# Last layer's experts: three projection pieces of 112, 112 and 64 + 64 columns, rows turned one part ahead, result reads in one row

## The chip, the core and the metric

The kernel runs on one core of a Trainium2 chip. A core has TensorE (PE; its weight loads are listed apart as PEld), VectorE (DVE), ScalarE (ACT), GpSimd (POOL) and SyncE (SP, which here only asks for transfers). They run at the same time and wait for each other through semaphores. The metric is the device time in microseconds (us) of one execution; lower is better. Everything is in fp32.

## What is computed

The program is a network of four layers on 4096 rows (16 sequences of 256) of 128 numbers. Each layer computes `x = x + s * silu(ffn(xn))`, where `xn` is the normalised `x`, `s` the output of the layer's mixer and `ffn` the layer's feed-forward part. The change touches only the feed-forward part of the last layer, a mixture of 16 experts with 2 experts per row and 640 places per expert, and one shared expert that all rows pass:

```python
def _mlp(h, wg, wu, wd):
    return jax.nn.silu(h @ wg) * (h @ wu) @ wd        # wg, wu: 128 x 176, wd: 176 x 128
...
expert_inputs = jnp.zeros((E, C, d), x.dtype).at[idx_flat, pos_c].add(x_pair)      # E = 16, C = 640
expert_outputs = jax.vmap(_mlp)(expert_inputs, w_gate, w_up, w_down)
gathered = expert_outputs[idx_flat, pos_c] * (vals_flat * within)[:, None]
output_tokens = gathered.reshape(N, K, d).sum(axis=1)
return x + _mlp(x, sw_gate, sw_up, sw_down) + output_tokens.reshape(b, s, d)
```

The hidden width is 176. An array of 128 columns takes it in two pieces.

## The kernel before

The last layer's mixer (a state-space scan, lines 1550 to 1960) ends at 3881 us. During it the rows of `xn` were already scattered to their experts' places in DRAM (`xd`, with the place to write back to and the router's weight in `md`). Then `ffn3` (line 1364) runs, in four stages:

- **Loads.** SP asks for the weights in groups (`weights`, lines 1374 to 1381: gate, up and down apart), for `mt`, and for the rows of the first experts (`rows_of`, line 1417; three buffers of 640 rows).
- **Shared expert** (lines 1427 to 1430). Eight chunks of 512 rows pass `mlp`; VectorE adds the result to `xn`.
- **Routed experts** (lines 1431 to 1446). Each expert's 640 rows are two parts: four tiles of 128 rows, and one. A part is transposed by TensorE into the PSUM tile `f3_pt` (line 1439), copied to SBUF by ScalarE as `f3_xT` (line 1441), passed through `mlp`, and scaled per row by VectorE into `f3_y` (line 1444). Then GpSimd issues five indirect writes, one for each 128 rows, to the rows' places in `yd` (`put_rows`, line 1359).
- **Tail** (lines 1449 to 1457). When all 80 indirect writes have landed, SP reads the two results of each row back in eight reads of 512 KB into `f3_r` (three buffers). For each, GpSimd adds the two (line 1454), VectorE adds `xn` (line 1455), and `gate` (lines 112 to 114) does silu on ScalarE, a product and a sum on VectorE; SP writes 256 KB of output.

`mlp` (lines 1383 to 1401) cuts the hidden width into two halves of 88, `j = 0, 1`. For each half one matmul makes the gate `pg` (line 1391) and one the up projection `pu` (line 1392), both with the half's 88 weight columns standing in the array and up to 512 rows streaming; ScalarE writes silu of `pg` to `h` (line 1393), VectorE multiplies `pu` into it (line 1394). Then for every 128 rows two matmuls, `j = 0` and `j = 1`, add up the down projection in `po` (line 1398): 88 rows of the array are used, 128 columns stream. An fp32 matmul appears in the trace as two passes, two LDWEIGHTS and two MATMUL records.

PSUM has eight banks here: two each for `f3_pg`, `f3_pu`, `f3_pt` and `f3_po`.

Nothing in `ffn3` fixes the order of instructions on an engine: the framework's scheduler sets it when the program is built. It prefers what is written first, but fills a wait that it foresees with later work that is ready. [...]

Of the kernel before, what the change touches and what calls it, by code (L numbers as in the profile page):

```python
# [8 lines left out]
F32 = mybir.dt.float32  # L9
AF = mybir.ActivationFunctionType  # L10
ALU = mybir.AluOpType
# [4 lines left out]
P = 128  # L16
B, S, D = 16, 256, 128
NT = B * S // P
NCH = B * S // 512
# [14 lines left out]
class Net:  # L34
# [1329 lines left out]
    def ffn3(self, xd, md, yd, sent):  # L1364


        nc, tc = self.nc, self.tc
        NE, F = 16, 88
        with ExitStack() as ctx:
            c = ctx.enter_context(tc.tile_pool(name="l3w", bufs=1))  # L1370
            sb = ctx.enter_context(tc.tile_pool(name="l3m", bufs=3))
            ps = ctx.enter_context(tc.tile_pool(name="l3m_ps", bufs=2, space=PSUM))

            def weights(lo, hi):

                t = []
                for n in ("wgate", "wup3", "wdown"):
                    src = self.a[n][:, lo:hi]
                    t.append(c.tile(list(src.shape), F32, name=f"{n}_{lo}"))
                    nc.sync.dma_start(t[-1], src)  # L1380
                return t

            def mlp(w, e, xT, n):

                wg, wu, wd = w
                h = sb.tile([F, 2, 512], F32, name="f3_h")
                for j in range(2):
                    f = slice(j * F, (j + 1) * F)
                    pg = ps.tile([P, 512], F32, name="f3_pg")
                    pu = ps.tile([P, 512], F32, name="f3_pu")  # L1390
                    nc.tensor.matmul(pg[:F, : n * P], lhsT=wg[:, e, f], rhs=xT, start=True, stop=True)  # L1391
                    nc.tensor.matmul(pu[:F, : n * P], lhsT=wu[:, e, f], rhs=xT, start=True, stop=True)  # L1392
                    nc.scalar.activation(h[:, j, : n * P], pg[:F, : n * P], AF.Silu)
                    nc.vector.tensor_tensor(h[:, j, : n * P], h[:, j, : n * P], pu[:F, : n * P], ALU.mult)
                po = ps.tile([P, 4, D], F32, name="f3_po")
                for k in range(n):
                    for j in range(2):
                        nc.tensor.matmul(  # L1398
                            po[:, k, :], lhsT=h[:, j, k * P : (k + 1) * P], rhs=wd[:, e, j, :], start=j == 0, stop=j == 1
                        )  # L1400
                return po

            sync = mybir.DependencyInfo(mybir.DependencyClass.Sync, mybir.DependencyReason.DATA)

            def fetch(out, src, scattered):
                d = nc.sync.dma_start(out, src)
                for q in scattered:
                    tc.add_manual_dep(d.ins, q.ins.name, sync, reason="scattered rows")

            shared = weights(NE, NE + 1)  # L1410
            mt = c.tile([P, NE, 5, 2], F32, name="f3_mt")
            fetch(mt, md[0 : 640 * NE, :].rearrange("(e p k) t -> p e k t", p=P, k=5), sent[1])
            to = c.tile([P, NE, 5], mybir.dt.int32, name="f3_to")
            nc.vector.tensor_copy(to, mt[:, :, :, 0])
            xs, ws, done = {}, {}, []

            def rows_of(e):
                x = xs[e] = sb.tile([P, 5, D], F32, name="f3_x")
                fetch(x, xd[640 * e : 640 * e + 640, :].rearrange("(p k) d -> p k d", k=5), sent[0])

            for e in range(2):
                if e == 0:
                    ws[0] = weights(0, 4)
                rows_of(e)
            for g in range(1, 4):
                ws[g] = weights(4 * g, 4 * g + 4)
            for t in range(NCH):
                k4 = slice(4 * t, 4 * t + 4)
                po = mlp(shared, 0, self.xnT[:, t * 512 : (t + 1) * 512], 4)
                nc.vector.tensor_tensor(self.xn[:, k4, :], po, self.xn[:, k4, :], ALU.add)  # L1430
            for e in range(NE):
                if e + 2 < NE:
                    rows_of(e + 2)
                x = xs.pop(e)
                y = sb.tile([P, 5, D], F32, name="f3_y", bufs=4)
                for k0, n in ((0, 4), (4, 1)):
                    pt = ps.tile([P, 4, P], F32, name="f3_pt")
                    for k in range(n):
                        nc.tensor.transpose(pt[:, k, :], x[:, k0 + k, :], self.ident)
                    xT = sb.tile([P, 512], F32, name="f3_xT")  # L1440
                    nc.scalar.copy(xT[:, : n * P], pt[:, :n, :].rearrange("p k d -> p (k d)"))
                    po = mlp(ws[e // 4], e % 4, xT[:, : n * P], n)
                    for k in range(n):
                        nc.vector.tensor_scalar_mul(y[:, k0 + k, :], po[:, k, :], mt[:, e, k0 + k, 1:2])
                for k in range(5):
                    self.put_rows(yd, to[:, e, k : k + 1], y[:, k, :], done)
            xo = self.out.rearrange("(k p) d -> p k d", p=P)
            back = yd[0 : 2 * B * S, :].rearrange("(p n j) d -> p n j d", n=NT, j=2)
            for t in range(NCH):
                k4 = slice(4 * t, 4 * t + 4)  # L1450
                r = sb.tile([P, 4, 2, D], F32, name="f3_r")
                fetch(r, back[:, k4], done)
                acc = sb.tile([P, 4, D], F32, name="f3_acc")
                nc.gpsimd.tensor_tensor(acc, r[:, :, 0, :], r[:, :, 1, :], ALU.add)
                nc.vector.tensor_tensor(acc, acc, self.xn[:, k4, :], ALU.add)
                self.gate(sb, acc, 4 * t, 4)
                nc.sync.dma_start(xo[:, k4, :], self.x[:, k4, :])


class Route3:  # L1460
# [4 lines left out]
    NE, CAP = 16, 640.0  # L1465
# [506 lines left out]
def layout(i):  # L1972
# [5 lines left out]
    i = {k: np.asarray(v) for k, v in i.items()}  # L1978
    p0, f0 = (lambda n: i["L0_attn_" + n]), (lambda n: i["L0_ffn_" + n])
    a = {"x": p0("x").reshape(B * S, D)}  # L1980
# [34 lines left out]
    for h in range(16):  # L2015
        o, m = 8 * h, h % 4
# [7 lines left out]
    p3, f3 = (lambda n: i["L3_attn_" + n]), (lambda n: i["L3_ffn_" + n])  # L2024
# [6 lines left out]
        a[d + "cb"], a[d + "dtb"], a[d + "D"] = (two(q(n))[:, :, 0] for n in ("conv_b", "dt_b", "D"))  # L2031
        a[d + "A"] = two(q("Alog")).reshape(P, 32)
    a["rw"], a["rb"] = f3("router_w"), row(f3("router_b"))
    for n, o in (("gate", "wgate"), ("up", "wup3")):
        a[o] = np.concatenate([f3("w_" + n), f3("sw_" + n)[None]], 0).transpose(1, 0, 2)
    a["wdown"] = np.concatenate([f3("w_down"), f3("sw_down")[None]], 0).reshape(17, 2, 88, D).transpose(2, 0, 1, 3)
    return {k: np.ascontiguousarray(v) for k, v in a.items()}


# [15 lines left out]
```

## Time and profile before

Three runs: 4092.97 us median (4090.22 to 4107.63).

| | |
|---|---|
| profiled execution, own time | 4101.38 us |
| its span from first to last instruction | 4099.7 us |
| granted TensorE clock over the span | 0.956 |
| span before `ffn3` (mixer's last write) | 0 to 3881 us |
| shared expert | 3881 to 3926 us |
| routed experts | 3926 to 4060 us |
| tail | 4060 to 4099.7 us |

In the rows of the profile, `L1391` is a line of the kernel. `f_pg<-f_xT,wgate 128*88 128x512` reads: from `f_xT` and `wgate` into `f_pg`; 128 rows and 88 columns of the array, 512 elements streamed. Brackets give the time that the engine was idle just before, and what ended it. In the timeline, consecutive instructions of one kind on one engine are merged (`x4`). The end of a matmul is modelled (a pass of 512 columns is given 592 ns though the next one starts 429 ns later), so the starts are what can be read.

| in `ffn3` | count | mean of one |
|---|---|---|
| gate and up matmul passes, 512 columns, routed (L1391, L1392) | 128 | next start after 0.43 us |
| the same, 128 columns | 128 | next start after 0.11 us |
| down passes, 128 columns (L1398) | 448 | next start after 0.11 us |
| silu of 512 columns (L1393, ACT) | 48 | 592 ns |
| product of 512 columns (L1394, DVE) | 48 | 684 ns |
| copy of transposed rows, 512 columns (L1441, ACT) | 16 | 585 ns |
| scaling of 128 rows (L1444, DVE) | 80 | 345 ns |
| indirect write of 128 rows (L1359, POOL) | 80 | 957 ns, and 0.30 us to the next |
| addition of two results (L1454, POOL) | 8 | 1403 ns |

### The profile page before, as it was taken

The numbers are of one execution on the slowest core, as the hardware profiler recorded it, in microseconds if no ns is written. First come the engines' busy times: TensorE is split into PE (matmuls) and PEld (weight loads), VectorE is DVE, ScalarE is ACT, GpSimd is POOL, SyncE is SP. The second block draws the span as 40 slices with busy tenths as digits, with TensorE's granted clock in tenths as the row PEclk, the third lists the DMA queues.
The fourth block names the chain that finished last, engine by engine and source line by source line (L and its number), as shares of the span: only waits on it lengthen the run. The fifth ranks groups of instructions, "written<-read, shape, count | busy, mean of one in ns | idle before, by whom it ended". The sixth has DMA issues, their size and how long they took to land. (4 is left out here: it accounts for less than half of the span.)

```text
span 4099.7 us, 61363 instructions
## 1 busy us (share of the span) xinstructions
PE 3617.1 (88%) x21623; PEld 2311.1 (56%) x21623; DVE 2983.6 (73%) x6273; ACT 2125.9 (52%) x4623; POOL 1914.6 (47%) x1932
## 2 busy tenths in 40 slices
PE   5689999875999999899999899998888889889895
PEld 3467777553566666677777677665333333333363
DVE  5567677575788887666666666757899899999834
ACT  2356666642777776344545333343566566566322
POOL 5974444000444444333333200121888988877634
PEclk8899999986999999999999999998999999999898
DMA  8365555320000000100000300000111121121123
GB/s 304 127 210 188 199 181 193 42 79 6 1 1 1 1 1 1 42 1 1 1 1 1 115 2 1 3 25 23 66 66 66 67 87 67 67 83 62 58 77 102
DMA packets 87366, 268.90 MB, mean 66 GB/s; under 512 B 18176, under 2 KB 34088, under 8 KB 81555
## 3 DMA queue, kind: packets, MB, share of 16 engines
q1 hardware_dynamic: 80403, 255.46, 18.4%
q0 software_dynamic: 6656, 9.52, 0.7%
q8 instruction: 172, 2.82, 0.3%
q14 instruction: 135, 1.11, 0.1%
HBM read 192.96 MB, written 71.97 MB: 65 GB/s over the span
## 5 line engine op out<-in xcount | busy, mean ns | idle before, releaser
L1829 POOL TENSOR_TENSOR m_h<-m_B,m_dtu 128x1024 f32<-128x1024 f32 x256 | 597.6, 2358 | 111.2 <-PE m_y L1959 62.0
L1855 DVE TENSOR_TENSOR_SCAN m_h<-m_a,m_h 128x512 f32<-128x512 f32 x512 | 600.8, 1207 | 43.9 <-ACT m_a L1844 34.8
L1959 PE MATMUL m_y<-m_h,ident 128*128 128x512 f32 x1024 | 519.5, 637 | 20.8 <-DVE m_h L1955 20.7
L883 POOL TENSOR_TENSOR a_e<-a_e,a_sm 128x512 f32<-128x512 f32 x256 | 263.5, 1040 | 448.3 <-DVE a_sm L882 354.5
L1118 DVE SCALAR_TENSOR_TENSOR f_acc<-f_po,f_gate,f_acc 128x128 f32<-128x128 f32 x1024 | 287.4, 344 | 164.3 <-PE f_po L1113 154.3
L1959 PEld LDWEIGHTS m_y<-m_h,ident 128*128 128x128 f32 x1024 | 185.7, 196 | 340.4 <-issue 251.0
L1113 PEld LDWEIGHTS f_po<-values_sb,f_h 128*128 128x128 f32 x2048 | 273.0, 195 | 158.9 <-issue 133.0
L398 DVE TENSOR_TENSOR a_e<-a_s,a_c 128x384 f32<-128x384 f32 x256 | 216.4, 846 | 191.2 <-PE a_s L395 188.5
L1190 POOL TENSOR_TENSOR r_g<-r_t 128x256 f32<-128x256 f32 x256 | 183.5, 728 | 359.3 <-DVE r_t L1189 356.0
L1221 ACT ACTIVATE r_e<-r_s,r_mx 128x256 f32<-128x256 f32 x512 | 207.4, 473 | 259.7 <-DVE r_mx L1215 259.7
L1955 DVE TENSOR_TENSOR m_h<-m_h,m_C 128x1024 f32<-128x1024 f32 x256 | 306.6, 1198 | 28.4 <-PE m_C L1865 28.4
L1083 ACT ACTIVATE f_h<-f_ph 128x512 f32<-128x512 f32 x256 | 152.1, 596 | 328.9 <-PE f_ph L1081 314.3
L1189 DVE TENSOR_TENSOR r_t<-r_pp,trig_sb 128x512 f32<-128x512 f32 x256 | 169.1, 681 | 207.3 <-PE r_pp L1180 206.1
L1113 PE MATMUL f_po<-values_sb,f_h 128*128 128x128 f32 x2048 | 276.8, 279 | 26.3 <-ACT f_h L1083 13.4
L876 ACT ACTIVATE a_e<-a_e,a_mx 128x256 f32<-128x256 f32 x512 | 255.0, 500 | 54.6 <-DVE a_sm L882 48.2
L1081 PE MATMUL f_ph<-xnT_sb,keys_sb 128*128 128x512 f32 x512 | 269.8, 610 | 0.4 <-ACT f_gate L1048 0.4
L403 ACT ACTIVATE a_e<-a_e,a_mx 128x128 f32<-128x128 f32 (+1 forms) x512 | 218.9, 453 | 87.7 <-DVE a_mx L399 62.0
L1209 PE MATMUL r_s<-pe_sb,r_g 128*128 128x256 f32 x1024 | 259.0, 386 | 0.0
L373 POOL COPY a_st<-a_p 128x192 f32<-128x192 f32 x256 | 135.1, 530 | 244.5 <-PE a_s L394 161.6
L1844 ACT ACTIVATE m_a<-m_dt,bA_sb 128x510 f32<-128x510 f32 x256 | 170.9, 686 | 141.3 <-DVE m_h L1855 140.4
L1865 PE MATMUL m_C<-m_dbc,ident 32*128 32x512 f32 x512 | 152.7, 670 | 99.0 <-DVE m_h L1955 91.2
L1844 ACT ACTIVATE m_a<-m_dt,fA_sb 128x510 f32<-128x510 f32 x256 | 169.9, 685 | 110.2 <-DVE m_h L1855 109.3
(476 smaller groups left out, 8199.1 us busy)
## 6 DMA issues: line engine op xcount, KB each, us to landing
m_B<-m_rows SPq DMA_DIRECT2D x32, 2048.0 KB
a_p<-pc SPq DMA_DIRECT2D x32, 768.0 KB
a_c<-cs SPq DMA_DIRECT2D x32, 768.0 KB
cs<-a_es SPq DMA_DIRECT2D x64, 256.0 KB
pc<-a_es SPq DMA_DIRECT2D x64, 256.0 KB
a_p<-pc SPq DMA_DIRECT2D x32, 512.0 KB
a_c<-cs SPq DMA_DIRECT2D x32, 512.0 KB
cs<-bg SPq DMA_DIRECT2D x8, 768.0 KB
```

The lines of the kernel that those rows point to most:

```text
L403: nc.scalar.activation(e[:, cols], e[:, cols], AF.Exp, bias=mx[:, i : i + 1])
L876: nc.scalar.activation(e[:, i, :], e[:, i, :], AF.Exp, bias=mx[:, i : i + 1], accum_out=sm[:, i : i + 1])
L883: nc.gpsimd.tensor_tensor(e, e, bc(sm, S), ALU.mult)
L1081: nc.tensor.matmul(ph, lhsT=keys[:, e, :], rhs=self.xnT[:, t * 512 : (t + 1) * 512], start=True, stop=True)
L1113: nc.tensor.matmul(po[:, k, :], lhsT=hT[:, k * P : (k + 1) * P], rhs=values[:, e, :], start=True, stop=True)
L1118: nc.vector.scalar_tensor_tensor(acc[:, n, :], po[:, k, :], gate[:, n, e : e + 1], acc[:, n, :], ALU.mult, ALU.add)
L1209: nc.tensor.matmul(s[h][:, i, :], lhsT=G[:, i * P : (i + 1) * P], rhs=w["pe"], start=False, stop=i == 1)
L1829: nc.gpsimd.tensor_tensor(h, st["B"][n // 8][:, m : m + 2, :], bc1(st["dtu"][:, k, :], 2), ALU.mult)
L1844: nc.scalar.activation(f[:, :, 1:], sts[d]["dt"][:, k, :].rearrange("p (b t) -> p b t", b=2)[:, :, 1:], AF.Exp, scale=w[work[d][1]]["A"][: ...
L1855: nc.vector.tensor_tensor_scan(h[:, j, :], ready.pop(0), h[:, j, :], 0.0, op0=ALU.mult, op1=ALU.add)
L1955: nc.vector.tensor_tensor(h, h, sts[d]["C"], ALU.mult)
L1959: nc.tensor.matmul(sts[d]["y"][k], lhsT=net.ident, rhs=h[:, j, :], start=False, stop=n + j == N - 1)
```

## The change

There are four edits.

1. **Pieces.** The hidden width is cut into 112 and 64 instead of 88 and 88. Gate and up weights lie in one tensor `wgu` of 352 columns: gate's first 112, up's first 112, gate's last 64, up's last 64. `mlp` issues three matmuls: `pg` and `pu` with 112 columns each, and `pc` with 128 columns, the upper half of which is the second gate piece and the lower half the second up piece. Silu and product work as before, on 112 and on 64 partitions. The down matmul of `j = 0` contracts over 112 rows of the array, that of `j = 1` over 64. The down weights are 112 partitions tall, zero-filled below the 64.
2. **Banks.** `pg`, `pu` and `pc` share one rotating set of four PSUM banks.
3. **Rows turned ahead.** Transposes and copy of a part are written one part earlier: those of part `i + 1` before `mlp` of part `i`. The read of the rows of expert `e + 2` moves with them. Each indirect write is written right after the scaling that it sends, instead of five after the expert.
4. **Tail.** The eight reads of the results are written in one row, into eight buffers, ahead of the eight chunks of work.

```diff
-        NE, F = 16, 88
+        NE, F = 16, (112, 64)
...
-                for n in ("wgate", "wup3", "wdown"):
+                for n in ("wgu", "wdown"):
...
-                wg, wu, wd = w
-                h = sb.tile([F, 2, 512], F32, name="f3_h")
-                for j in range(2):
-                    f = slice(j * F, (j + 1) * F)
-                    pg = ps.tile([P, 512], F32, name="f3_pg")
-                    pu = ps.tile([P, 512], F32, name="f3_pu")
-                    nc.tensor.matmul(pg[:F, : n * P], lhsT=wg[:, e, f], rhs=xT, start=True, stop=True)
-                    nc.tensor.matmul(pu[:F, : n * P], lhsT=wu[:, e, f], rhs=xT, start=True, stop=True)
-                    nc.scalar.activation(h[:, j, : n * P], pg[:F, : n * P], AF.Silu)
-                    nc.vector.tensor_tensor(h[:, j, : n * P], h[:, j, : n * P], pu[:F, : n * P], ALU.mult)
+                wgu, wd = w
+                h = sb.tile([F[0], 2, 512], F32, name="f3_h")
+                pg, pu, pc = (ps.tile([P, 512], F32, name="f3_pi", bufs=4)[:, : n * P] for _ in range(3))
+                pg, pu = pg[: F[0]], pu[: F[0]]
+                for p, o in ((pg, 0), (pu, F[0]), (pc, 2 * F[0])):
+                    nc.tensor.matmul(p, lhsT=wgu[:, e, o : o + p.shape[0]], rhs=xT, start=True, stop=True)
+                for j, (g, u) in enumerate(((pg, pu), (pc[: F[1]], pc[F[1] :]))):
+                    hj = h[: F[j], j, : n * P]
+                    nc.scalar.activation(hj, g, AF.Silu)
+                    nc.vector.tensor_tensor(hj, hj, u, ALU.mult)
                 po = ps.tile([P, 4, D], F32, name="f3_po")
...
-                            po[:, k, :], lhsT=h[:, j, k * P : (k + 1) * P], rhs=wd[:, e, j, :], start=j == 0, stop=j == 1
+                            po[:, k, :], lhsT=h[: F[j], j, k * P : (k + 1) * P], rhs=wd[: F[j], e, j, :], start=j == 0, stop=j == 1
...
+            parts = [(e, k0, n) for e in range(NE) for k0, n in ((0, 4), (4, 1))]
+            ahead = turned(*parts[0])
+            for i, (e, k0, n) in enumerate(parts):
+                xT = ahead
+                if i + 1 < len(parts):
+                    ahead = turned(*parts[i + 1])
+                if k0 == 0:
+                    y = sb.tile([P, 5, D], F32, name="f3_y", bufs=4)
+                po = mlp(ws[e // 4], e % 4, xT, n)
+                for k in range(n):
+                    nc.vector.tensor_scalar_mul(y[:, k0 + k, :], po[:, k, :], mt[:, e, k0 + k, 1:2])
+                    self.put_rows(yd, to[:, e, k0 + k : k0 + k + 1], y[:, k0 + k, :], done)
...
-            for t in range(NCH):
+            rs = [sb.tile([P, 4, 2, D], F32, name="f3_r", bufs=NCH) for _ in range(NCH)]
+            for t, r in enumerate(rs):
+                fetch(r, back[:, 4 * t : 4 * t + 4], done)
+            for t, r in enumerate(rs):
                 k4 = slice(4 * t, 4 * t + 4)
-                r = sb.tile([P, 4, 2, D], F32, name="f3_r")
-                fetch(r, back[:, k4], done)
```

`turned(e, k0, n)` holds the transposes, the copy and, for `k0 == 0`, the read of expert `e + 2`, as they stood in the loop.

More of the change, by code (lines that the diff above doesn't have):

```diff
@@ L1430, in ffn3, with turned @@
                 nc.vector.tensor_tensor(self.xn[:, k4, :], po, self.xn[:, k4, :], ALU.add)
-            for e in range(NE):
-                if e + 2 < NE:
+            def turned(e, k0, n):
+                if k0 == 0 and e + 2 < NE:
                     rows_of(e + 2)
[L1434 to L1446, printed above, removed]
+                pt = ps.tile([P, 4, P], F32, name="f3_pt")
+                for k in range(n):
+                    nc.tensor.transpose(pt[:, k, :], xs[e][:, k0 + k, :], self.ident)
+                xT = sb.tile([P, 512], F32, name="f3_xT")
+                nc.scalar.copy(xT[:, : n * P], pt[:, :n, :].rearrange("p k d -> p (k d)"))
+                return xT[:, : n * P]
@@ new lines, in ffn3 @@
+            parts = [(e, k0, n) for e in range(NE) for k0, n in ((0, 4), (4, 1))]
[7 more added lines that the diff above has]
+                po = mlp(ws[e // 4], e % 4, xT, n)
+                for k in range(n):
+                    nc.vector.tensor_scalar_mul(y[:, k0 + k, :], po[:, k, :], mt[:, e, k0 + k, 1:2])
+                    self.put_rows(yd, to[:, e, k0 + k : k0 + k + 1], y[:, k0 + k, :], done)
@@ L2033, in layout @@
     a["rw"], a["rb"] = f3("router_w"), row(f3("router_b"))
-    for n, o in (("gate", "wgate"), ("up", "wup3")):
-        a[o] = np.concatenate([f3("w_" + n), f3("sw_" + n)[None]], 0).transpose(1, 0, 2)
-    a["wdown"] = np.concatenate([f3("w_down"), f3("sw_down")[None]], 0).reshape(17, 2, 88, D).transpose(2, 0, 1, 3)
+    g, u, v = (np.concatenate([f3("w_" + n), f3("sw_" + n)[None]], 0) for n in ("gate", "up", "down"))
+    a["wgu"] = np.concatenate([t[:, :, o] for o in (slice(0, 112), slice(112, None)) for t in (g, u)], 2).transpose(1, 0, 2)
+    a["wdown"] = np.zeros((112, 17, 2, D), v.dtype)
+    a["wdown"][:, :, 0] = v[:, :112].transpose(1, 0, 2)
+    a["wdown"][:64, :, 1] = v[:, 112:].transpose(1, 0, 2)
     return {k: np.ascontiguousarray(v) for k, v in a.items()}
```

## The prediction

> **What bounds the kernel now.** I first cut the span with the view of windows at the stages of `ffn3`:
>
> ```profile
> core 0: us, PE busy (x) PEld busy (x) DVE busy (x) ACT busy (x) POOL busy (x), PEclk, DMA share, GB/s
> ...
> 3881.00:3926.00 45.00, 42.63 (x183) 23.55 (x183) 16.08 (x25) 9.48 (x16) 0.00 (x0) 0.96 0.46 127
> 3926.00:4060.00 134.00, 122.81 (x671) 81.70 (x669) 54.27 (x146) 39.73 (x96) 73.29 (x77) 1.00 0.24 70
> 4060.00:4100.00 40.00, 0.00 (x0) 0.00 (x0) 21.45 (x24) 5.04 (x8) 14.48 (x12) 0.53 0.53 164
> ```
>
> Only the last 219 of 4099.7 us can change. In the shared and the routed stage PE is the busy engine (95% and 92%); in the tail it does nothing. One period of the routed loop, from the timeline, shows where PE's other time goes:
>
> ```profile
> 4032.96 0.71 PE L1439 MATMUL f_pt<-ident,f_x 128*128 128x128 f32 x5
> 4033.65 0.75 ACT L1441 COPY f_xT<-f_pt 128x512 f32<-128x512 f32 x2 [2.46 <-PE f_pt L1439]
> ...
> 4034.29 1.09 PE L1391 MATMUL f_pg<-f_xT,wgate 128*88 128x512 f32 x2 [0.62 <-ACT f_xT L1441]
> ...
> 4035.44 1.02 PE L1392 MATMUL f_pu<-f_xT,wup 128*88 128x512 f32 x2
> ...
> 4036.30 1.02 PE L1391 MATMUL f_pg<-f_xT,wgate 128*88 128x512 f32 x2
> ...
> 4037.16 1.02 PE L1392 MATMUL f_pu<-f_xT,wup 128*88 128x512 f32 x2
> ...
> 4039.03 1.83 PE L1398 MATMUL f_po<-wdown,f_h 88*128 88x128 f32 x14
> ...
> 4041.14 0.71 PE L1439 MATMUL f_pt<-ident,f_x 128*128 128x128 f32 x5
> ```
>
> Read the starts. A projection of 512 columns takes 0.86 us (4035.44 to 4036.30); one of 128 columns takes 0.22 us by the same reading. From one `f_pt` row to the next is 8.18 us. PE's work in it, by starts: 4 x 0.86 + 4 x 0.22 for the projections, 20 passes of the down projection at 0.11 (2.22), five transposes (0.56): **7.1 us**. The missing 1.1 us is mostly one place: after the transposes PE waits for ScalarE's copy, 0.62 us in the bracket and about 0.16 hidden in the modelled end of the last transpose. In the shared stage the period is 5.25 us, the work 4 x 0.86 + 16 x 0.11 = 5.2: no wait worth having.
>
> **Pieces, the gain.** Three projections instead of four, and the time of a pass doesn't depend on its standing columns (128 x 512 passes of L1740 and 88-column ones both have a mean of 592 ns). Saved: 0.86 + 0.22 = 1.08 us for each of 16 experts, 17.2 us; 0.86 for each of eight shared chunks, 6.9 us. 24.1 us of PE.
>
> **Pieces, the price.** The down projection now alternates between 112 and 64 rows of the array. The 88-row passes of today run like 128-row ones (next start after 0.11 us). A 64-row matmul is different. The trace has one of the same form, K = 64 from partition 0, between 128-row neighbours:
>
> ```profile
> 3717.63 1.02 PE L1959 MATMUL m_y<-m_h,ident 128*128 128x512 f32 x2
> 3718.58 0.29 PEld L1772 LDWEIGHTS m_pp<-m_dbc,fdtT_sb 64*128 64x128 f32 x2 [0.76 <-ACT m_a L1844]
> 3718.59 1.12 PE L1772 MATMUL m_pp<-m_dbc,fdtT_sb 64*128 64x512 f32 x2
> ...
> 3719.64 1.98 PE L1959 MATMUL m_y<-m_h,ident 128*128 128x512 f32 x4
> ```
>
> Two 128-row passes take 0.86 us. Here two of them followed by the switch take 0.96, and the two 64-row passes with the switch back 1.05: **0.29 us more for a pair**. The weight row says why: the load begins at 3718.58, together with the matmul, not one pass ahead. Its second pass has no load ahead either (starts 533 ns apart, against 429). At 128 columns the single starts agree: 205 ns into 64 rows, 201 out of them, against 109. Every 128 rows of input pay this once: 5 x 0.29 = 1.45 us an expert, 32 x 0.29 = 9.3 us in the shared stage. That is 32.5 us of PE, more than the 24.1 saved.
>
> [...]
>
> **Rows turned ahead.** The copy of the next part is then finished long before its projections, so the 0.78 us at each expert goes. What is late next is the second piece of `h`. Before, the last projection (`pu`) was followed only by its product, because silu of `pg` ran beside it. Now `pc` carries both: its second pass starts 2.15 us after `pg`'s first, silu starts 0.66 later (by today's rows), takes 0.59, the product 0.68, with 0.1 between: `h` is whole at 4.2 us while PE has nothing of its own part from 2.6 on but one down pair (0.22). To fill 1.6 us there are that pair, the next expert's four transposes (0.45) and the three 128-column projections (0.65): 1.3. I take 0.3 us of waiting. PE per expert: 3 x 0.86 + 3 x 0.22 + 5 x 0.73 + 0.56 + 0.3 = **7.75**, against 8.18: 0.43 x 16 = **-6.9 us**. In the shared stage the next chunk's `pg` and `pu` (1.72) more than fill the gap; the fourth bank is free for `pg`, and `pu` takes the bank that silu has left. Period 3 x 0.86 + 4 x 0.73 = 5.5 against 5.25: **+1.9 us** over eight.
>
> Costs at nothing, and their cover: VectorE and ScalarE do the same number of operations at the same lengths (54 and 40 of 134 us busy). The moved reads of rows wait for the same three buffers; they are issued one part earlier and the rows are far ahead. The indirect writes stay 80, each 0.96 + 0.30 = 1.26 us of POOL, 6.3 us per expert: hidden under 7.75, and they already start after the first scaling (4058.16, scaling at 4057.53). SP's weight loads lose a transfer per group; the first now brings all 352 columns before `pg` can start: between 0 and 0.5 us later, I take **+0.2**.
>
> **Tail.** The reads asked for at once end POOL's waits (15.1 us of idle before L1454). But VectorE and POOL exclude each other here:
>
> ```profile
> 4069.35 4.19 POOL L1454 TENSOR_TENSOR f_acc<-f_r 128x512 f32<-128x512 f32 x3 [5.18 <-DMA f_r<-f_yd]
> 4070.64 1.78 DVE L1455 TENSOR_TENSOR f_acc<-f_acc,xn_sb 128x512 f32<-128x512 f32 x1 [10.86 <-POOL f_acc L1454]
> ...
> 4093.76 0.69 DVE L114 TENSOR_TENSOR x_sb<-x_sb,gate_t 128x512 f32<-128x512 f32 x1
> ```
>
> A VectorE addition alone takes 0.68; begun beside a POOL addition it takes 1.78. One after the other, 8 x 1.26 and 24 x 0.60 (their pitch) are 24.5 us; from the first addition to the last product it is 25.1 today. So at most 0.6 can go, and a worse order can cost as much. I take **-0.5**.
>
> **Sum.** -6.9 + 1.9 + 0.2 - 0.5 = -5.3 us: 4101.4 becomes 4096.1 for a profiled execution, 4093.0 becomes **4088** for the median. With every wait gone it would be -10; with 0.3 us more waiting per expert, 0. With the spread of runs (17 us over three), the likeliest case's own range is 4076 to 4100. What a measurement here tells from no change is about 0.5%, 20 us.
>
> **Rivals.**
> *The 64-row pieces cost nothing extra.* For it: 88-row passes cost nothing, and scheduling may hide a load. Against it: the four rows above. PE would need 6.0 us, POOL's writes 6.3 would become the bound; at 6.35, (8.18 - 6.35) x 16 = 29, shared (5.25 - 4.36) x 8 = 7, tail 0.5: 4056. Chance 0.11.
> *The gap after `pc` isn't filled* (slower). The fixed order puts the short projections and transposes elsewhere, and PE waits at both stages until 4.2 us. Expert: 4.2 + the 2.7 of down work left + 0.73 + 1.2 = 8.8; shared 6.9. 0.65 x 16 + 1.64 x 8 = +23: 4116. For it: today's order already puts `f_pg` ahead of a ready down pair and waits for the copy. Against it: in the shared stage it filled the same gap without a wait. It decides once waiting exceeds the 0.3 I gave by 0.33 us per expert. Chance 0.10.
> [...] Chance 0.06.
> The likeliest case keeps 0.73.
>
> **How the numbers follow.** Faster by over 0.5%: the first rival, and 0.05 for runs that come out well: 0.16. Slower by over 0.5%: the second, and 0.03: 0.13. The rest, 0.71. The range 4064 to 4110 leaves out the centres of those two.
>
> **What would show it.** A row `f_po` of `64*128`, with weight loads that begin with their matmul; expert period by the `f_pg` starts near 7.75, shared chunk near 5.5; no idle bracket `ACT f_xT` before `f_pg`, but one `DVE f_h` before `f_po`; POOL without DMA waits in the tail, its span still near 25 us. I am wrong if the 64-row passes start 0.11 apart, if the expert period is below 7 or above 8.5, or if the tail shortens by several us.

## The result and the profile after

The changed kernel takes **4111.79 us** (median of 5 runs, 4109.38 to 4120.68) against 4097.22 us (4090.22 to 4107.63) for the kernel before on the same chip: a ratio of 1.0039, 95% interval 1.0023 to 1.0055. It is slower, by 14.6 us by the medians and 16 by the ratio. That is still inside the 0.5% that the prediction called no change; but the prediction said 5 us faster, and its range ended at 4110.

The profiled execution took 4111.4 us, its span is 4109.7. The windows at the stages of `ffn3`, with the columns that the prediction showed (engines in the order PE, PEld, DVE, ACT, POOL, each with its instructions in brackets, then PE's clock, then DMA):

```profile
3881.00:3926.00 45.00, 44.44 (x172) 25.44 (x171) 14.78 (x22) 9.51 (x17) 0.00 (x0) 1.00 0.35 104
3926.00:4060.00 134.00, 134.00 (x542) 80.03 (x542) 49.33 (x131) 33.38 (x89) 67.00 (x70) 0.89 0.21 64
4060.00:4110.00 50.00, 11.32 (x48) 7.06 (x48) 26.45 (x39) 6.75 (x12) 21.89 (x18) 0.61 0.40 139
```

Two things in the second row. PE is busy in all of the 134 us and yet gets through 542 matmul passes, where it did 671 before. Only a part of that is by design: an expert has 37 passes now and had 41, so the same pace would give about 606. And the granted clock is 0.89; before it was 1.00. Hardly a wait of PE is left, and the stage is longer.

Stages are best compared from event to event, since what comes before them differs from run to run. By the starts and ends in the traces, in us:

| | before | after | predicted change |
|---|---|---|---|
| shared: first projection to last addition into `xn` | 45.5 | 52.0 | +1.9 and +0.2 |
| routed: from there to the last scaling of `f_y` | 130.6 | 144.5 | -6.9 |
| tail: from there to the end | 39.9 | 37.7 | -0.5 |
| sum | 216.0 | 234.2 | -5.3 |

So `ffn3` costs 18.2 us more. (The spans differ by 10.0 only: in these two executions the layers ahead of `ffn3`, which the change doesn't touch, took 3883.7 us before and 3875.5 after. The section at the end comes back to that.)

The chain of waits shows the routed loop as one run of PE instructions, start and length:

```profile
3956.52 3.75 PE f_po L1398 x18
3960.27 2.76 PE f_pi L1390 x6
3963.03 0.48 PE f_po L1398 x2
3963.51 0.44 PE f_pt L1437 x4
3963.95 0.66 PE f_pi L1390 x6
3964.61 0.11 PE f_pt L1437
3964.71 3.81 PE f_po L1398 x18
3968.52 4.35 PE f_pi L1390 x6
3972.87 0.48 PE f_po L1398 x2
```

One expert is three 512-column projections (`f_pi` x6), one down pair, transposes, three 128-column projections, one transpose and nine down pairs (`f_po` x18). From 3956.52 to 3964.71 it takes 8.19 us; 7.75 was predicted. Of it, the eighteen down passes take 3.75, **0.21 us for each**; before, the 88-row passes took 0.11. The six projection passes behind the second stretch take 4.35 us instead of 2.76. They are the same six instructions, at half the clock. Windows of 3.41 us there show it (the figure after the five engines is the clock):

```profile
3961.46:3964.87 3.41, 3.41 (x19) 2.06 (x17) 1.42 (x3) 1.91 (x6) 2.78 (x3) 1.00 0.18 58
3964.87:3968.28 3.41, 3.41 (x18) 2.43 (x17) 1.15 (x5) 0.23 (x2) 0.96 (x1) 1.00 0.45 137
3968.28:3971.70 3.42, 3.42 (x6) 1.40 (x5) 0.77 (x3) 0.60 (x1) 2.80 (x3) 0.50 0.12 38
```

The stretch of down passes, then 3.41 us at a clock of 0.50, right after it. The routed stage has nine such windows, at 3934, 3968, 3978, 3996, 4006, 4016, 4033, 4043 and 4054 us; the kernel before has none there. Each of them lasts 3.413 us, and every other record of the granted clock in this trace, but for the last, which ends with the run, lasts a whole multiple of that; a piece of this length is called a clock window below.

The groups by form, with the idle time ahead of each at the end of the row:

```profile
L1398 PE MATMUL f_po<-wdown,f_h 64*128 64x128 f32 x224 | 55.6, 329 | 0.3 <-DVE f_h L1394 0.3
L1398 PE MATMUL f_po<-wdown,f_h 112*128 112x128 f32 x224 | 54.2, 324 | 0.0
L1390 PE MATMUL f_pi<-f_xT,wgu 128*112 128x512 f32 x64 | 45.1, 842 | 0.6 <-ACT f_xT L1439 0.6
```

Waiting for the second piece of `h` is 0.3 us in all, over 16 experts and 8 chunks; 0.3 for each expert was predicted. And the 112-row passes are as long as the 64-row ones.

### The profile page after: what moved, and what is told of

Read it like the earlier page. It is cut to its first block, busy times and chain, and to the rows that moved or that the text cites. A ratio compares the mean times of both kernels' runs of the same rounds, so it can differ in the third digit from the quotient of the medians.

```text
span 4109.7 us, 61157 instructions
## 1 busy us (share of the span) xinstructions
PE 3650.0 (89%) x21543; PEld 2324.5 (57%) x21543; DVE 2982.2 (73%) x6273; ACT 2121.7 (52%) x4623; POOL 1915.7 (47%) x1932
## 5 line engine op out<-in xcount | busy, mean ns | idle before, releaser
L1967 PE MATMUL m_y<-m_h,ident 128*128 128x512 f32 x1024 | 519.6, 637 | 20.8 <-DVE m_h L1963 20.6
```

The lines of the kernel that those rows point to most:

```text
L1967: nc.tensor.matmul(sts[d]["y"][k], lhsT=net.ident, rhs=h[:, j, :], start=False, stop=n + j == N - 1)
```

## The experiments

Two explanations stood against each other at first. One: what costs is that the array changes between 112 and 64 rows, and the slow passes also bring the clock down. The rival: the cost lies in the new order (rows turned ahead, four shared banks, writes one by one), or the clock falls for a reason that has nothing to do with the rows. Eight kernels, each of which keeps the layers ahead of `ffn3` as they are. In the table the stages are cut as above; medians and ratios are against the kernel before on the same chip (4097.22 us, 5 runs, for the changed kernel; 4097.7, 20 runs, for `pad` to `pieces`; 4093.08, 13 runs, for the others).

| | shared | routed | tail | sum | median | ratio, 95% interval |
|---|---|---|---|---|---|---|
| before | 45.5 | 130.6 | 39.9 | 216.0 | | |
| after | 52.0 | 144.5 | 37.7 | 234.2 | 4111.79 | 1.0039 (1.0023 to 1.0055) |
| `pad` | 39.8 | 99.8 | 39.0 | 178.5 | 4060.18 | 0.9904 (0.9875 to 0.9933) |
| `split` | 52.0 | 125.4 | 37.9 | 215.3 | 4098.22 | 1.0000 (0.9984 to 1.0016) |
| `nopieces` | 45.5 | 117.8 | 36.5 | 199.9 | 4081.43 | 0.9954 (0.9934 to 0.9973) |
| `pieces` | 52.0 | 144.4 | 40.2 | 236.6 | 4116.21 | 1.0041 (1.0025 to 1.0057) |
| `tail` | 45.5 | 130.6 | 36.7 | 212.7 | 4089.45 | 0.9988 (0.9979 to 0.9998) |
| `pad65` | 39.8 | 99.8 | 38.9 | 178.5 | 4056.66 | 0.9909 (0.9893 to 0.9926) |
| `pairs` | 56.1 | 128.9 | 37.7 | 222.6 | 4116.86 (one run) | |
| `padpairs` | 37.5 | 99.7 | 41.1 | 178.3 | 4059.07 (one run) | |

The differences of the sums and of the medians agree to 4 us in each row that has both, so the stages can be trusted.

**`pad`: the second down piece over all 112 rows.** Same three pieces, same order; the second half of `h` lies in three fixed buffers whose rows 64 to 112 are zero, and so are those rows of the down weights.

```diff
+            hs = [c.tile([F[0], 2, 512], F32, name=f"f3_h{i}") for i in range(3)]
+            for t in hs:
+                nc.vector.memset(t[F[1] :, 1, :], 0.0)
+            turn = []
...
-                h = sb.tile([F[0], 2, 512], F32, name="f3_h")
+                h = hs[len(turn) % 3]
+                turn.append(1)
...
-  lhsT=h[: F[j], j, k * P : (k + 1) * P], rhs=wd[: F[j], e, j, :]
+  lhsT=h[:, j, k * P : (k + 1) * P], rhs=wd[:, e, j, :]
```

> The changed kernel, with the down projection's second piece contracted over all 112 array rows (h's rows 64 to 112 are set to zero once, in three fixed buffers; the weights are zero there already). Same number of matmuls, no 64-row mode. Theory A (the passes through the 64-row mode cost 0.2 us instead of 0.11, and the sparse 3.75 us they make together lets the TensorE clock fall to half in the next 3.4 us window): passes of the down projection 0.11 apart, no half-clock window in the routed stage, expert period 6.3 to 6.6 (then GpSimd's five writes of 1.26 us decide), shared period 4.4; about 55 us below the changed kernel, near 4055. Rival B (the cost is the order, the shared set of banks or the wait for h after pc): the period stays above 7.5 and the time above 4095. Rival C (the clock windows come by themselves): at least five half-clock windows stay in the routed stage.

Measured: 4060.18 us, 52 us below the changed kernel, with the same number of matmuls, the same projections and the same order. Its chain of waits, one expert:

```profile
3954.35 2.01 PE f_po L1404 x18
3956.36 2.58 PE f_pi L1396 x6
3958.94 0.48 PE f_po L1404 x2
3959.42 0.44 PE f_pt L1443 x4
3959.85 0.66 PE f_pi L1396 x6
3960.51 0.11 PE f_pt L1443
3960.62 2.01 PE f_po L1404 x18
```

The eighteen passes take 2.01 us instead of 3.75, and the expert 6.27 instead of 8.19. More rows of the array are at work, and it is faster. The windows of the shared and of the routed stage:

```profile
3881.00:3921.00 40.00, 39.43 (x187) 24.91 (x185) 17.23 (x26) 10.85 (x19) 0.00 (x0) 0.96 0.50 152
3921.00:4021.00 100.00, 97.83 (x582) 69.82 (x581) 52.99 (x144) 35.00 (x93) 72.37 (x76) 1.00 0.28 90
```

The clock in the routed stage is back at 1.00. So both the long passes and the half clock come with the 64 rows. The fixed buffers for `h` are a second difference, but they can hardly be the cause: the changed kernel waits for `h` only 0.3 us in all, and the 64-row passes of the layer ahead, which have no such buffers, pay the same price (shown below). What is next is POOL: in the timeline of `pad` its indirect writes follow each other with 0.30 us between and 0.96 each, without a longer gap; 5 x 1.26 = 6.3 us is the expert. PE's chain is as long (6.27), so which of the two would bind a faster kernel isn't shown.

**`split`: the order of the down projection.** As after, but the down projection of an expert's last 128 rows is written behind the next expert's 512-column projections; nothing else differs, the 64-row passes are as many.

```diff
-                po = mlp(ws[e // 4], e % 4, xT, n)
-                for k in range(n):
-                    nc.vector.tensor_scalar_mul(y[:, k0 + k, :], po[:, k, :], mt[:, e, k0 + k, 1:2])
-                    self.put_rows(yd, to[:, e, k0 + k : k0 + k + 1], y[:, k0 + k, :], done)
+                h = mlp(ws[e // 4], e % 4, xT, n)
+                if k0 == 0:
+                    if late:
+                        finish(*late.pop())
+                    finish(e, k0, n, h, y)
+                else:
+                    late.append((e, k0, n, h, y))
+            finish(*late.pop())
```

`finish` holds the down projection, the scaling and the writes.

> The changed kernel with the same matmuls in the same modes, but the down projection of an expert's last 128 rows is written after the next expert's 512-column projections. The sparse stretch shrinks from 18 passes (3.75 us) to 14 (2.9 us), under one clock window of 3.4 us. Theory A (a window wholly inside a sparse stretch halves the clock for the next): no half-clock window in the routed stage, period about 7.9 at all experts, about 20 us below the changed kernel, near 4090. Rival D (the mean load of TensorE sets the clock, not the length of a stretch): the half-clock windows stay at about nine and the time within 7 us of the changed kernel.

Measured: 4098.22, ratio 1.0000; 13.6 us below the changed kernel by the medians, where theory A had said about 20. The shared stage is as slow as after (52.0), the routed one 19 us shorter. Its timeline, PE alone:

```profile
3958.64 1.22 PE L1403 MATMUL f_po<-wdown,f_h 112*128 112x128 f32 x6
...
3960.14 0.82 PE L1390 MATMUL f_pi<-f_xT,wgu 128*112 128x128 f32 x6
3960.89 2.98 PE L1403 MATMUL f_po<-wdown,f_h 64*128 64x128 f32 x14
...
3963.97 2.74 PE L1390 MATMUL f_pi<-f_xT,wgu 128*112 128x512 f32 x6
```

The down passes now come as 6 and 14 in place of 2 and 18. From start to start the expert is 7.90 us. The long stretch lasts 2.9 us, less than 3.41, and there is no half clock in the stage:

```profile
3935.00:4060.00 125.00, 124.18 (x583) 81.94 (x581) 54.72 (x144) 36.69 (x93) 72.82 (x76) 1.00 0.22 72
```

So most of what `split` wins is the clock: the slow passes are as many as before it.

**`nopieces` and `pieces`: the two halves of the change.** `nopieces` is the changed kernel with the old four pieces of 88 columns and the old banks, and so with rows turned ahead, writes one by one and the tail in one row. `pieces` is the kernel before with edits 1 and 2 alone.

`nopieces` against after:

```diff
-        NE, F = 16, (112, 64)
+        NE, F = 16, 88
```

`pieces` against before:

```diff
-        NE, F = 16, 88
+        NE, F = 16, (112, 64)
```

`mlp`, the names of the weights and their packing go with these lines, as in the diff of the change.

> Before's four projections of 88 columns and two down pieces of 88 rows, with the rows turned ahead and the tail's reads in one row. Theory A: no half-clock window, period 7.3 to 7.6, routed stage about 10 us shorter than before, tail 2 us: about 4085, 12 below before. Rival C (turning ahead itself packs the stretch so that the clock falls): half-clock windows in the routed stage, not faster than before.

> Before with the three pieces alone: rows turned in place, tail as before. Theory A: the wait for the copy stays (0.6 to 0.8 us per expert) and the down passes are 0.2 apart: period 8.8 to 9.0 without windows, more with them; 15 to 35 us above before, 4112 to 4132. Rival B (turning ahead or the tail is what lost): within 5 us of before or below.

Measured: `nopieces` 4081.43, 16 us faster than before; `pieces` 4116.21, 18 us slower. The pieces alone are the loss, and the rest of the change is a gain that they eat. With four pieces, edit 3 (turning ahead, and the writes one by one; the two weren't tried apart) is worth 12.8 us in the routed stage (130.6 to 117.8). With three it is worth nothing (144.4 and 144.5). The timeline of `pieces` says why:

```profile
3949.13 0.83 PE L1390 MATMUL f_pi<-f_xT,wgu 128*112 128x128 f32 x6
3949.80 0.71 PE L1439 MATMUL f_pt<-ident,f_x 128*128 128x128 f32 x5
3950.43 4.25 PE L1398 MATMUL f_po<-wdown,f_h 64*128 64x128 f32 x18
3954.61 2.71 PE L1390 MATMUL f_pi<-f_xT,wgu 128*112 128x512 f32 x3
```

The next expert's transposes already stand ahead of the eighteen down passes, though the text writes them in the next turn of the loop. The order on PE isn't the order of the text; the scheduler had found that place by itself. The copy then runs beside the down passes: in the routed stage of `pieces`, from 3930 us on, the long projections wait 0.0 us for it, so nothing is left to remove. The expectation that this wait stays was wrong. The stage has nine half-clock windows, as after.

**`tail`: the reads in one row, alone.** The kernel before with edit 4.

> Before with the tail's eight reads in one row and eight buffers alone. From the changed kernel's trace (37.7 us from the last scaling to the end, against 39.9): 1 to 3 us less in the tail, everything ahead of it unchanged (period 8.18, no half-clock window in the routed stage), within 4 us of before. The prediction's floor (VectorE and GpSimd one after the other, 24.5 us from the first addition to the last sum) would leave 0.6 us at most.

Measured: 4089.45, ratio 0.9988, a gain of 3.6 us by the medians and 3.2 in the stage. The timeline of the changed kernel's tail (`SPq` is the queue of SP's DMAs):

```profile
4078.44 3.91 SPq L1406 DMA_DIRECT2D f_r<-f_yd  x8
4082.30 5.85 POOL L1462 TENSOR_TENSOR f_acc<-f_r 128x512 f32<-128x512 f32 x4 [5.23 <-DMA f_r<-f_yd]
4083.59 1.77 DVE L1463 TENSOR_TENSOR f_acc<-f_acc,xn_sb 128x512 f32<-128x512 f32 x1 [11.62 <-POOL f_acc L1462]
...
4104.52 1.29 DVE L114 TENSOR_TENSOR x_sb<-x_sb,gate_t 128x512 f32<-128x512 f32 x2
```

From the first addition to the end of the last product it is 23.5 us, against 25.1 before, and from there to the end 3.9 against 5.25.

**`pad65`: one row of zeros.** As `pad`, with 65 rows in the contraction instead of 112.

```diff
-                nc.vector.memset(t[F[1] :, 1, :], 0.0)
+                nc.vector.memset(t[F[1] : F[1] + 1, 1, :], 0.0)
...
-  lhsT=h[:, j, k * P : (k + 1) * P], rhs=wd[:, e, j, :]
+  lhsT=h[: (112, 65)[j], j, k * P : (k + 1) * P], rhs=wd[: (112, 65)[j], e, j, :]
```

> The padded kernel with the second down piece contracted over 65 rows instead of 112 (one zero row). If the mode is chosen by 64 rows or fewer: the same as the padded kernel, down passes 0.11 apart, period 6.28, near 4060. If every row count under 128 that differs from the neighbour's costs a switch: passes 0.2 apart, period near 7.9, above 4085.

Measured: 4056.66, and the stages of `pad` to 0.1 us. Its groups of down passes, with modelled means of 281 and 274 ns as `pad`'s 279:

```profile
L1404 PE MATMUL f_po<-wdown,f_h 112*128 112x128 f32 x224 | 44.9, 281 | 0.0
L1404 PE MATMUL f_po<-wdown,f_h 65*128 65x128 f32 x224 | 43.4, 274 | 0.3 <-DVE f_h L1400 0.3
```

The starts of the down passes in its trace are mostly 109 to 114 ns apart, between 112 and 65 rows and within each. So it isn't that the second piece is small, nor that the number of rows changes: 65 rows run as 112 do, 64 don't. That there is a "mode", and that fewer rows than 64 would share it, is the author's estimate in the expectations; what the runs show is the two paces, 0.11 and 0.21 us, and no run has the second piece over fewer than 64 rows.

**`pairs` and `padpairs`: is it the length of the sparse stretch?** `pairs` is `split` with the shared chunks taken two at a time: six projections of 512 columns for both, then the down projections of both, 32 passes in one stretch. Their order on PE is held by dependencies that carry no wait. `padpairs` is the same over all 112 rows.

```diff
-            for t in range(NCH):
-                k4 = slice(4 * t, 4 * t + 4)
-                po = mlp(shared, 0, self.xnT[:, t * 512 : (t + 1) * 512], 4)
-                nc.vector.tensor_tensor(self.xn[:, k4, :], po, self.xn[:, k4, :], ALU.add)
+            for t in range(0, NCH, 2):
+                hs = [mlp(shared, 0, self.xnT[:, q * 512 : (q + 1) * 512], 4) for q in (t, t + 1)]
+                seen["hold"] = seen["pc"]
+                for q, h in zip((t, t + 1), hs):
+                    k4 = slice(4 * q, 4 * q + 4)
+                    po = down(shared, 0, h, 4)
+                    nc.vector.tensor_tensor(self.xn[:, k4, :], po, self.xn[:, k4, :], ALU.add)
+                seen["after"] = seen["po"]
```

> The split kernel (no half-clock window in its shared or routed stage) with the shared expert's chunks done in pairs: six projections, then 32 down passes in one stretch of about 6.6 us. The same instructions. Theory A (a clock window of 3.4 us wholly inside the sparse stretch halves the clock for the next window): three or four half-clock windows in the shared stage, each beginning inside or just behind a stretch, and 3 to 7 us more in this stage than split's 47.2. Rival D (the mean load over the stage sets the clock): none, and the stage within 2 us of 47.2. Routed stage as split, 130.

> The same pairs of chunks with the down passes padded to 112 rows: 32 passes of 0.11 us, a stretch of 3.6 us, longer than a clock window too. Theory A in its exact form (what counts is how sparse the stretch is, not that its passes are short): no half-clock window, shared stage within 2 us of the padded kernel's 36.4 (plus the waits for h that pairs bring). Rival E (any stretch of 128-column passes longer than a window halves the clock): at least two half-clock windows in the shared stage.

Measured: one run each, so they are read by their stages. (The expectations cut the shared stage shorter: `split`'s 47.2 and `pad`'s 36.4 there stand beside 52.0 and 39.8 in the table.) `pairs` has four half-clock windows behind the one at the beginning and takes 4.1 us more than `split`, as theory A had said. The shared stage of `split` had no half clock but at its beginning; that of `pairs` has it again and again. Its timeline, and windows of 4 us:

```profile
3914.28 6.79 PE L1408 MATMUL f_po<-wdown,f_h 112*128 112x128 f32 x32
```

```profile
3900.00:3904.00 4.00, 4.00 (x20) 2.81 (x19) 1.38 (x2) 0.19 (x1) 0.00 (x0) 0.94 1.02 328
3904.00:3908.00 4.00, 4.00 (x12) 2.75 (x12) 0.15 (x1) 0.00 (x0) 0.00 (x0) 0.50 1.04 299
...
3916.00:3920.00 4.00, 4.00 (x20) 2.80 (x20) 0.69 (x1) 0.00 (x0) 0.00 (x0) 1.00 0.00 0
3920.00:3924.00 4.00, 4.00 (x9) 2.02 (x9) 0.69 (x1) 0.60 (x1) 0.00 (x0) 0.58 0.00 0
```

PE is busy in every microsecond, nothing waits, and the clock falls 4 us after the first long stretch began and 6 us after the second. In the second pair no DMA moves at all (last two columns), so memory traffic isn't the reason. `padpairs` keeps a clock of 1.00 over the same order; its stretch from 3903.37 us to 3906.94 covers nearly a whole clock window (3903.62 to 3907.03):

```profile
3904.00:3908.00 4.00, 4.00 (x31) 3.48 (x31) 2.07 (x3) 0.16 (x1) 0.00 (x0) 1.00 0.00 0
3912.00:3916.00 4.00, 4.00 (x36) 3.90 (x35) 1.71 (x4) 0.59 (x1) 0.00 (x0) 1.00 0.01 4
```

Length and sparseness were both needed in these runs: short and sparse (`split`, 2.9 us with passes 0.21 us apart) keeps the clock, long and dense (`padpairs`, 3.57 us, 0.11 us apart) keeps it, long and sparse (`pairs`, 6.8 us, 0.21 us apart) loses it. But sparse means two things at once here, passes further apart and, in half of them, fewer rows; these two runs don't separate them, and the last section says what other windows of the traces show.

Not tried: all down passes over 112 rows of an expert ahead of all those over 64, which would leave two changes per expert instead of ten. And no run has passes 0.21 us apart over all 112 rows.

## Why the prediction was wrong

Two steps of the prediction failed. In "Pieces, the price" a pair of down matmuls was put at 0.29 us more, where it costs 0.39: over 112 pairs (80 of the experts, 32 of the shared one), 11 us. And the clock was taken as 1.00 without a reason, where half-clock windows cost about 14 us. Added to the predicted 4088, either of them alone would have stayed within the range (4099 or 4102); both make 4114, with 4111.79 measured. One of its own signs of being wrong, an expert period above 8.5, came too: 144.5 / 16 is 9.0 on average, 8.19 for an expert without half clock.

**The price of a pair of down matmuls** was the first term that was off. The prediction took 0.29 us, or 0.73 us per 128 rows; it is 0.39, or 0.83. The starts in the trace after are 204 ns from a 112-row pass to a 64-row one, 213 to its second pass, 201 back to 112 rows, and 212 to that one's second pass. The prediction had the first three and took 0.11 for the last. The trace of before had the fourth too, in a line that the prediction shows: `m_y` x4 at 3719.64 lasts 1.98 us, where four passes at 429 ns with the modelled end of 592 are 1.88. The next 64-row row is

```profile
3721.55 1.12 PE L1772 MATMUL m_pp<-m_dbc,fdtT_sb 64*128 64x512 f32 x2
```

From 3718.59 to 3721.55 six passes take 2.96 us instead of 6 x 0.43 = 2.58: 0.39 more. The reading stopped at the switch back, one pass too early. The 0.06 in the forecast was the chance of a pair dearer than 0.29, a value of the author's estimate that no run shows; measured is 0.39. The trace shows where the time goes: where nothing changes, the weight load of a pass begins with the matmul before it, 0.11 us ahead (`pad`, load at 3954.301, its matmul at 3954.410). At a change it begins with its own matmul, 0.20 us after the one before (3957.279 and 3957.281, after 3957.076); the second pass's load begins 0.11 us behind the first load (3957.388), and its matmul another 0.11 us later (3957.495). So of both passes the load no longer runs ahead as far as it did, in either direction of the change. Why a change does that, the trace doesn't say.

In the shared stage a chunk takes 5.91 us, not 5.5: 8 x 0.41 = 3.3 of the 4.4 us by which it missed (the last chunk takes another 0.5, the rest isn't worked out). In the routed stage the twenty passes of an expert take 3.75 + 0.48 = 4.23 instead of 3.65, its six long projections 2.76 where `pad` has 2.58, and the 0.3 us of waiting falls away: 8.19 instead of 7.75, 16 x 0.44 = 7.0 us.

**The clock** isn't in the prediction, in no step and no rival. Nine windows at half speed, each worth about 4.35 - 2.76 = 1.6 us, are 14.3 us; with the 7.0 that is 21.3, against the 20.8 by which the routed stage missed. `split` takes the half clock away and leaves the passes, and is 19 us faster there, where 14.3 and its shorter period, 16 x 0.29 = 4.6, make 18.9. The prediction had read a clock of 1.00 for this stage and let it stand for a kernel that feeds PE in another rhythm.

**The gain of the pieces** was right: `pad` has it without the price, and `nopieces` is the same without the pieces. The two are 5.7 us apart in the shared stage and 18.0 in the routed one, 23.7 together, where 24.1 was predicted. With the other edits `pad` is 37.5 us faster in `ffn3` than before. The first rival, with 64-row pieces that cost nothing, had given 4056 with POOL's writes as the next bound. That is what `pad` and `pad65` do; only 64 rows don't do it.

**Rows turned ahead** were said to be worth 0.78 us an expert, 12.5 in all, beside the pieces. With the old pieces they are worth 12.8, with the new ones nothing. The order in `pieces` suggests why: the transposes went by themselves into the gap after `pc`, and with them the wait that was to be saved. That doesn't show in the miss as a term of its own, since the predicted period was built from PE's work and not from the difference.

**The wait for `h`**: 0.3 us an expert predicted, 0.3 in the whole stage measured. The work named as cover was enough. The slower rival, in which that gap stays open, had named 4116; its number comes close by luck, and its mechanism doesn't occur.

**The tail**: -0.5 predicted, -2.2 measured, and -3.2 alone. The floor of 24.5 us was too high by 1.0, and the last output's way out, not counted, is 1.35 us shorter. Against it, the time from the end of the last scaling to the start of the last indirect write grew by 0.7, from 3.43 to 4.15.

**The sum**: -5.3 was the small rest of a gain of 37 us (`pad` against before) and a loss that came out at 56 (`pad` against after). A tenth of a microsecond in one term, taken for each of 112 times 128 rows, is 11 us, twice the forecast; the range should have carried it.

## What to carry to other kernels

A contraction of 64 rows between larger ones is best padded (fewer rows weren't tried): one row of zeros (65 rows) kept every pass at 0.11 us where 64 rows had all four passes of the pair at 0.21. After a change that makes TensorE's passes sparser, look at its granted clock even if it never idles, and break sparse stretches so that they stay shorter than a clock window, here 3.41 us (14 slow passes, 2.9 us, kept the clock in `split`; 18 of them, 3.75 us, lost it nine times over the 16 experts); and read a price from one whole period of the nearest row, up to the same instruction again, not up to where the odd one ends. Before building an order by hand, see whether the scheduler already has it.

## What the hardware showed beside that

**A busy TensorE can lose its clock.** Every half-clock stretch in the routed stage of the changed kernel is one clock window, 3.41 us long. It doesn't take an idle PE: in that stage no pass starts more than 0.99 us after the one before it, and nine windows fell. So busy isn't the measure. Take the share of a window in which columns stream, an estimate from the starts in which a 128-column pass counts as 0.107 us, a quarter of the 429 ns at which 512-column passes follow one another. In the changed kernel, `pieces`, `pairs` and `split` it is 0.50 to 0.56 in the full-clock windows of these loops that were followed by half clock and 0.54 and up in those that were not; `pad` doesn't go below 0.74 while its loops run. But that alone doesn't separate the windows either. In an earlier layer of the kernel before, windows with eight passes of 128 columns and two of 512, all over 128 rows, have shares of 0.50 and 0.42, and the clock stays:

```profile
2727.83:2731.24 3.41, 1.99 (x10) 1.19 (x10) 1.37 (x4) 0.34 (x1) 1.98 (x3) 1.00 0.07 20
2731.24:2734.66 3.42, 1.61 (x10) 1.20 (x11) 2.88 (x10) 1.09 (x2) 0.00 (x0) 1.00 0.00 0
2734.66:2738.07 3.41, 3.41 (x21) 2.65 (x21) 2.39 (x10) 1.19 (x2) 0.00 (x0) 1.00 0.01 2
```

PE idles for more than a third of the first two windows and keeps its clock; with 3.41 of 3.41 us busy at 3964.87, above, it lost it. What fits both is the share with each pass weighted by its rows (64 of 128 count as half), again an estimate. In the ten traces, all 339 full-clock windows with less than 0.36 were followed by half clock, 47 of 270 between 0.36 and 0.42, and 4 of 10,109 with more. The slow passes, over 112 and 64 rows at 0.21 us, have 0.35. So the rows at work seem to count, and `pad` mended both: its passes are closer together and over more rows. That weighting is inferred from the windows; no run here put passes this far apart over more rows.

**The clock ahead of the change differs from run to run.** The first shared projection starts between 3866.8 us (`nopieces`) and 3892.5 (`pairs`) in the ten traces, though the layers before it are the same. The time at half clock ahead of it goes from 307 to 372 us in the same two; half of the difference is 32 us, enough for the 26 (in between the two don't always go together: the kernel before starts at 3883.7 with 321 us). A single span of this kernel can't tell 10 us, a stage measured between two of its own events can.
